# A planner's durations of a norm, and a new table for its ties, in a fused Mamba and MLP kernel

## The chip, the cores and the metric

The kernel runs on one core of a Trainium2 chip. The metric is the time of one execution on the device, in microseconds. A time given as a result is the median of several executions. A profile is one further execution, recorded by the hardware profiler: its span runs from the first to the last instruction.

TensorE (PE in the views) does the matmuls, and PEld is its loading of weights. VectorE is DVE, ScalarE is ACT, GpSimd is POOL, and SyncE is SP, which here only issues DMA transfers. Each engine has a queue of its own and takes its instructions in the order of the program. Engines wait for each other by semaphores.

## The reference

The input is 8 images of 384 channels and 32 by 32 points, so 1024 tokens each. A first branch is a state-space layer with an MLP, a second is an MLP with binarised weights whose outputs are quantised. Cut to what matters (the names are shortened):

```python
# 1: state space and MLP, all 8 images
t = layernorm(ln_c(x)) * ln_w + ln_b               # over 384 channels
xm, z = split(t @ in_proj_w.T)                     # 768 each
xc = silu(causal_conv(xm, 3 taps) + conv_b)
dt, Bm, Cm = split(xc @ x_proj_w.T)                # 24, 16, 16
dt = softplus(dt @ dt_proj_w.T + dt_proj_b)
h[l] = exp(dt[l] * A) * h[l-1] + dt[l] * xc[l] * Bm[l]   # 768 x 16 states, 1024 steps
y = (sum_n h * Cm + xc * D) * silu(z)
t = y @ out_proj_w.T
x = x + gelu(t @ mlp_w1.T + mlp_b1) @ mlp_w2.T + mlp_b2
# 2: per image, for the first 5 images (the other 3 pass through)
h = quantise(ln_t(x) @ sign(W1 - group mean).T + b1)     # 1536; absmax over the image
x = x + quantise(gelu(h) @ sign(W2 - group mean).T + b2)
```

## The kernel before

Everything is float32. An image is worked in two halves of 512 tokens (`T`), with the channels on the 128 partitions. Per image b there are a front part `s1` (norm, input projection, convolution, `dt`), the scan `s2`, an output part `s3` (output projection and MLP), and for b < 5 a second MLP `ffn`. What passes between the parts goes through DRAM.

The scan runs as exponentials on ScalarE (`da`), products on GpSimd (`u`, L992), prefix scans on VectorE (L1017) and sums over the 16 states on TensorE (`py`, L956). It takes most of the time of those three engines. The projections (`p_in`, `p_z`, `p_out`, `p_h`, `p_o`, `p_y`: L568) take most of TensorE's.

**Who orders the work.** The parts are not run as they are written. Each operation is recorded by `Plan.add` with an engine, a planned cost in microseconds, and what it reads and writes. When all are recorded, `Plan.run` plays them through once, on the host, when the program is built. It keeps a clock of its own for each engine, takes at each step the engine that can start earliest, lets `choose` pick one of the operations that are ready there, and emits it. So the planned costs decide nothing but the order of each engine's queue, and the host for those operations that may run on two engines (the `others` of `add`). The chip then follows that order with its true durations.

Where several operations are ready, `rank` sorts them: by a class for the part of the kernel, by the image, and then by the order of recording. The last is disturbed on purpose, by the table `TURNS` (L93), which has one number for each 100 us (`STRETCH`) of the planner's clock and 0 past its end:

```python
at = int(now / STRETCH)
turn = TURNS[at] if at < len(TURNS) else 0
...
by = turn & 0xFFFF
return (*first, op.prio[2] + (turned(op.prio[2], by) if by else 0))
```

`turned` makes a shift between -16 and +16 out of the operation's number and `by`, as a hash does. The bits above 65535 are flags for the stretch. `LATE_FRONTS` ranks the front parts behind the output parts. `DVE_SCANS` and `POOL_SCANS` let VectorE or GpSimd take the operations of the scan first; without them they come behind other work that is ready. `ACT_STAGES` holds ScalarE to operations outside of the scan that need no change of its function table.

If the planner's TensorE would be idle for more than 0.7 us (`IDLE`), it puts in filler matmuls of 256 columns, `spare` (L478), whose results nobody reads.

**The norm** (`norm`, 26 groups of it: 16 in the front parts, 10 in `ffn`) is a round trip over all engines, and TensorE has four steps of it. `total` adds three blocks of channels, on GpSimd in two additions (L655, L656) or on VectorE in one reduction (L659). `p_mean` (L667) is a matmul with ones, which sums over the partitions and spreads the sum. VectorE subtracts the mean (L670), ScalarE squares, and `p_var` (L626, helper `columns`) sums the squares in 12 small matmuls on a quarter of the array each. An eviction brings `var` to SBUF and `p_turned` (L681) transposes it. VectorE adds the epsilon (L685), GpSimd takes the power -0.5 (L687), `p_r` (L644, helper `spread`) spreads it in 4 matmuls, and VectorE multiplies (L691). The 4 matmuls `p_r` can't start before the power is there, and whatever stands behind them in TensorE's queue waits as well.

PSUM has three buffers (`mm`) for the matmuls' results; a matmul can't start until one of them has been emptied by ScalarE or VectorE (`affine`: L597, L599, L604, L606).

Of the kernel before, what the change touches and what calls it, by code (L numbers as in the profile page):

```python
# [35 lines left out]
KC = C // P  # L36
# [8 lines left out]
T = 512  # L45
# [26 lines left out]
MM = 0.859  # L72
# [18 lines left out]
STRETCH, REACH = 100, 16  # L91
LATE_FRONTS, DVE_SCANS, POOL_SCANS, ACT_STAGES = 1 << 16, 1 << 17, 1 << 18, 1 << 19
TURNS = (  # L93
    59965, 29935, 54697, 25830, 41556, 52704, 5806, 54013, 24204, 552223,
    25982, 47623, 34875, 16007, 24111, 42172, 43083, 15421, 638691, 11540,
    33479, 220645, 233617, 13861, 59336, 49176, 14182, 227647, 59245, 317456,
)


# [9 lines left out]
def c_act(n):  # L109
    return 0.2 + n * 0.00084  # L110


def c_dve(n):
    return 0.17 + n * 0.00102
# [90 lines left out]
class Plan:  # L205
# [12 lines left out]
    def add(self, engine, cost, emit, r=(), w=(), claim=(), table=None, size=0, others=None,  # L218
            land=1.6, rate=350e3, lag=None, tiled=False):
        op = Op()  # L220
        op.engine, op.cost, op.emit, op.table = engine, cost, emit, table
        op.others, op.settle = others or {}, None
        op.size, op.land, op.prio = 0.03 + size / rate, land - 0.1, (*self.prio, len(self.ops))
        op.next, op.ready, op.tiles, op.tiled = [], 0.0, [], tiled
        op.lag = LAG.get(engine, 0.0) if lag is None else lag
        op.slack = SLACK if self.prio[0] < 0 else 0.0
        deps = set()

        def parts_of(t):
            t, part = t if isinstance(t, tuple) else (t, None)  # L230
            if t not in op.tiles:
                op.tiles.append(t)
                if t.ring is not None:
                    t.left += 1
            if part is None:
                if None not in t.parts:
                    t.parts[None] = [None, []]
                return list(t.parts.values())
            if part not in t.parts:
                whole = t.parts.get(None)  # L240
                t.parts[part] = [whole[0], list(whole[1])] if whole else [None, []]
            return [t.parts[part]]

        for t in claim:
            t.left += 1
            op.tiles.append(t)
        for t in r:
            for p in parts_of(t):
                if p[0] is not None:
                    deps.add(p[0])  # L250
                p[1].append(op)
        for t in w:
            for p in parts_of(t):
                if p[0] is not None:
                    deps.add(p[0])
                deps.update(p[1])
                p[0], p[1] = op, []
        deps.discard(op)
        op.wants = len(deps)
        for d in deps:  # L260
            d.next.append(op)
        self.ops.append(op)
        return op
# [154 lines left out]
class Layer:  # L418
# [198 lines left out]
    def norm(self, t, eps, scale):  # L617

        nc, add = self.nc, self.plan.add
        def columns(src, name):  # L620
            p = self.piece("mm", [P, TG], name)

            def emit():
                for k in range(KC):
                    for g in range(G):
                        nc.tensor.matmul(  # L626
                            p.real[g * DQ : (g + 1) * DQ, :], self.ones[:, :DQ],
                            src.real[:, k, g * TG : (g + 1) * TG],
                            start=(k == 0), stop=(k == KC - 1),
                        )  # L630

            add("PE", 0.79, emit, r=[src], w=[p], tiled=True)
            return p

        def spread(src, name, turned=False):
            p = self.piece("mm", [P, T], name)

            def emit():
                for g in range(G):
                    if turned:  # L640
                        by, of = src.real[:, g : g + 1], self.ident
                    else:
                        by, of = self.ident[:, g * DQ : g * DQ + 1], src.real
                    nc.tensor.matmul(  # L644
                        p.real[:, g * TG : (g + 1) * TG], by.to_broadcast([P, P]), of,
                        start=True, stop=True,
                    )

            add("PE", 0.89, emit, r=[src], w=[p])
            return p  # L650

        total = self.piece("sq", [P, T], "total")

        def in_two():
            nc.gpsimd.tensor_add(total.real, t.real[:, 0, :], t.real[:, 1, :])  # L655
            nc.gpsimd.tensor_add(total.real, total.real, t.real[:, 2, :])  # L656

        def at_once():
            nc.vector.tensor_reduce(  # L659
                total.real, t.real.rearrange("p k l -> p l k"), AX.X, ALU.add  # L660
            )

        add("POOL", 2.5, in_two, r=[t], w=[total], others={
            "DVE": (c_dve(KC * T) + 0.02, at_once)
        })
        p_mean = self.piece("mm", [P, T], "p_mean")
        add("PE", MM, lambda: nc.tensor.matmul(  # L667
            p_mean.real, self.ones, total.real, start=True, stop=True
        ), r=[total], w=[p_mean])
        add("DVE", c_dve(KC * T) + 0.05, lambda: nc.vector.scalar_tensor_tensor(  # L670
            t.real, p_mean.real.unsqueeze(1).to_broadcast([P, KC, T]), -1.0 / C, t.real,
            ALU.mult, ALU.add,
        ), r=[p_mean], w=[t])

        sq = self.piece("sq", [P, KC, T], "sq")
        self.act(lambda: sq.real, lambda: t.real, AF.Square, c_act(KC * T), r=[t], w=[sq])
        p_var = columns(sq, "p_var")
        var = self.piece("rstd", [P, TG], "var")
        self.affine(lambda: var.real, lambda: p_var.real, [p_var], [var], scale=scale, n=TG)
        p_turned = self.piece("mm", [P, G], "p_turned")  # L680
        add("PE", 0.14, lambda: nc.tensor.matmul(  # L681
            p_turned.real, var.real, self.ident[:, ::DQ], start=True, stop=True
        ), r=[var], w=[p_turned])
        rstd = self.piece("root", [P, G], "rstd")
        add("DVE", 0.15, lambda: nc.vector.tensor_scalar_add(rstd.real, p_turned.real, eps),  # L685
            r=[p_turned], w=[rstd])
        add("POOL", 1.0, lambda: nc.gpsimd.tensor_tensor(  # L687
            rstd.real, rstd.real, self.power.to_broadcast([P, G]), ALU.pow
        ), w=[rstd])
        p_r = spread(rstd, "p_r", True)  # L690
        add("DVE", c_dve(KC * T), lambda: nc.vector.tensor_mul(  # L691
            t.real, t.real, p_r.real.unsqueeze(1).to_broadcast([P, KC, T])
        ), r=[p_r], w=[t])
# [738 lines left out]
```

## Time and profile before

| what | time |
|---|---|
| median of 3 runs | 3130.09 us (3128.02 to 3130.24) |
| the profiled execution | 3132.08 us |
| its span | 3130.3 us |
| granted TensorE clock, mean | 0.993 |
| fillers `spare` (L478), 119 matmuls | 58.6 us busy on TensorE |
| `p_var`, 26 groups of 12 matmuls | 22.0 us busy |
| `p_r`, 26 groups of 4 matmuls | 31.2 us busy |
| `p_mean`, 26 matmuls | 29.4 us busy |
| `total` on GpSimd, first and second addition | 1.28 and 1.27 us each |
| `total` on VectorE | 1.91 us each |

A matmul in float32 leaves two records in the trace, as it passes the array twice. Busy time of a group is the time in which at least one of its instructions ran. The span is less than the time of the execution by what lies around the first and the last instruction, 1.8 us here.

### The profile page before, as it was taken

The page shows a single profiled execution, that of the slowest core. Times are in us where ns is not written, and L with a number is a line of the kernel's source. Part 1 is how long each engine was busy: PE and PEld are TensorE (multiplying, and loading weights), DVE is VectorE, ACT ScalarE, POOL GpSimd, SP SyncE. Part 2 cuts the span into 40 slices and gives each one's busy share as a digit, 9 for nine tenths or more (in the row PEclk, how much of TensorE's full clock was granted, in tenths as well). Part 3 has the DMA queues.
Part 4 walks back from the last instruction along what each step waited for, and adds up shares of the span by engine and source line. Part 5 has one row for each costly group of instructions (what it writes and reads, how often), then busy time and mean ns, then how long its engine had stood idle before and what let it go on. Part 6 is the DMA issues. An engine that isn't in the chain of part 4 may idle for free.

```text
span 3130.3 us, 32297 instructions
## 1 busy us (share of the span) xinstructions
PE 3049.4 (97%) x10202; PEld 1243.8 (40%) x10202; DVE 2599.5 (83%) x2053; ACT 2019.1 (65%) x2406; POOL 2802.1 (90%) x1095
## 2 busy tenths in 40 slices
PE   9899999999999999999999999999999999999999
PEld 4334333333333444434343334343334444333334
DVE  4787888999987889878799888898788988798880
ACT  4887787776576566667666665666745556666562
POOL 2889888999999998999989998999999999999880
PEclk9999999999999999999999999999999999999999
DMA  7999778777787667777679675886877756756442
GB/s 231 305 312 314 241 255 282 272 251 254 256 318 241 207 202 259 280 263 259 202 256 319 206 231 194 298 276 211 269 250 229 238 187 220 243 187 211 155 152 73
DMA packets 348969, 751.76 MB, mean 240 GB/s; under 512 B 36480, under 2 KB 113792, under 8 KB 339584
## 3 DMA queue, kind: packets, MB, share of 16 engines
q1 hardware_dynamic: 348368, 749.61, 71.9%
q8 instruction: 82, 1.34, 0.2%
q14 instruction: 87, 0.71, 0.1%
q10 hardware_dynamic: 432, 0.09, 0.0%
HBM read 569.21 MB, written 180.36 MB: 239 GB/s over the span
## 4 chain that ended last, share of the span: by engine, by line
PE 53%; DVE 6%; DMA 5%; ACT 5%; POOL 4%; issue 2%; SPq 0%; DVEq 0%; POOLq 0%; ACTq 0%
PE p_y L568 16%; PE p_o L568 11%; PE p_h L568 9%; PE py L956 7%; PE p_out L568 5%; POOL u L992 3%; DVE u L1017 2%; PE p_in L568 2%; DVE da L1017 2%; PE p_z L568 2%; ACT da L584 1%; ACT L584 1%; DMA w_b<-in_mlp_w 1%; DMA w<-in_mlp_w 1%; DMA w_n<-bin_w 1%
## 5 line engine op out<-in xcount | busy, mean ns | idle before, releaser
L584 ACT ACTIVATE da<-dt_r,a_neg 128x1024 f32<-128x1024 f32 (+1 forms) x960 | 898.2, 944 | 559.4 <-DVE u L1017 292.1
L992 POOL TENSOR_TENSOR u<-dtx_r,bc 128x2048 f32<-128x2048 f32 (+1 forms) x360 | 1186.4, 3311 | 75.7 <-PE py L956 38.8
L1017 DVE TENSOR_TENSOR_SCAN u<-da,u 128x1024 f32<-128x1024 f32 (+1 forms) x436 | 871.2, 2009 | 165.7 <-POOL u L992 77.7
L992 POOL TENSOR_TENSOR u<-u,bc 128x2048 f32<-128x2048 f32 (+1 forms) x274 | 900.0, 3290 | 74.4 <-DVE u L1017 68.0
L568 PE MATMUL p_h<-t,w_b 128*128 128x512 f32 x1152 | 513.1, 597 | 10.7 <-DMA w_b<-in_mlp_w 5.0
L568 PE MATMUL p_o<-g,w 128*128 128x512 f32 x1152 | 512.3, 597 | 7.5 <-DMA w<-in_mlp_w 5.7
L1017 DVE TENSOR_TENSOR_SCAN da<-da,dtx_r 128x1024 f32<-128x1024 f32 (+1 forms) x192 | 380.4, 2014 | 51.1 <-POOL dtx_r L992 31.4
L992 POOL TENSOR_TENSOR dtx_r<-dtx_r,bc 128x2048 f32<-128x2048 f32 (+1 forms) x120 | 397.0, 3312 | 1.8
L568 PEld LDWEIGHTS p_o<-g,w 128*128 128x128 f32 x1152 | 214.6, 190 | 299.7 <-issue 271.1
L568 PE MATMUL p_y<-gf,w_n 128*128 128x512 f32 x720 | 323.5, 601 | 9.3 <-DMA w_n<-bin_w 6.0
L568 PEld LDWEIGHTS p_h<-t,w_b 128*128 128x128 f32 x1152 | 213.9, 190 | 298.1 <-issue 259.8
L568 PE MATMUL p_y<-tn,w_b 128*128 128x512 f32 x720 | 318.9, 597 | 3.2 <-DVE rstd L685 2.5
L956 PE MATMUL py<-u,fold 128*32 128x512 f32 x2304 | 303.2, 625 | 0.0
L1017 DVE TENSOR_TENSOR_SCAN da<-da,u 128x1024 f32<-128x1024 f32 (+1 forms) x140 | 280.8, 2037 | 11.7 <-ACT da L584 10.8
L584 ACT ACT_TABLE_LOAD x213 | 273.3, 1283 | 5.5 <-DMA dt_r<-dt_d 1.8
L568 PE MATMUL p_out<-yg,w 128*128 128x512 f32 x552 | 245.5, 596 | 2.1 <-DMA w<-in_out_proj_w 1.3
L568 PE MATMUL p_in<-t,w_f 128*128 128x512 f32 x504 | 230.6, 606 | 12.6 <-issue 5.2
L568 PE MATMUL p_z<-t,w_f 128*128 128x512 f32 x504 | 227.1, 599 | 2.0 <-issue 1.0
L568 PEld LDWEIGHTS p_y<-gf,w_n 128*128 128x128 f32 x720 | 134.1, 191 | 196.0 <-issue 173.4
L568 PEld LDWEIGHTS p_y<-tn,w_b 128*128 128x128 f32 x720 | 134.4, 190 | 184.5 <-issue 167.0
L1037 DVE TENSOR_TENSOR dtx_r<-da,bc 128x1024 f32<-128x1024 f32 x144 | 170.8, 1214 | 0.1
L599 ACT ACTIVATE g<-p_h,v_vecs 128x512 f32<-128x512 f32 x159 | 107.5, 678 | 89.9 <-PE p_h L568 89.4
(131 smaller groups left out, 3152.4 us busy)
## 6 DMA issues: line engine op xcount, KB each, us to landing
dtx_r<-dtx_d SPq DMA_DIRECT2D x72, 1024.0 KB, 5.9
dt_r<-dt_d SPq DMA_DIRECT2D x144, 512.0 KB, 5.1
w_b<-in_mlp_w SPq DMA_DIRECT2D x192, 192.0 KB, 3.5
w<-in_mlp_w SPq DMA_DIRECT2D x96, 384.0 KB, 3.4
w_f<-in_in_proj_w SPq DMA_DIRECT2D x168, 192.0 KB, 4.4
y_d<-y SPq DMA_DIRECT2D x120, 256.0 KB, 4.9
gf<-y_d SPq DMA_DIRECT2D x60, 512.0 KB, 6.3
xc_d<-xc SPq DMA_DIRECT2D x48, 512.0 KB, 6.1
```

The lines of the kernel that those rows point to most:

```text
L568: self.nc.tensor.matmul(p.real, w.real[:, w0 + k, :], t.at(k0 + k), start=start and k == 0, stop=stop and k == n - 1,)
L584: lambda: self.nc.scalar.activation(out(), in_(), func, **{k: v() if callable(v) else v for k, v in kw.items()}),
L599: nc.scalar.activation(out(), in_(), AF.Identity, bias=bias, scale=scale)
L956: nc.tensor.matmul(py.real[g * DQ : (g + 1) * DQ, :], self.fold, hc, start=False, stop=(q == NQUAD - 1), skip_group_check=True,)
L992: nc.gpsimd.tensor_mul(u.real[:, x], t.real[:, x], row.real.unsqueeze(2).to_broadcast([P, n, 2]))
L1017: da=da, in_u=in_u: nc.vector.tensor_tensor_scan(to(i), da.real[:, i, :], in_u(i), state.real[:, col : col + 1] if half else 0.0, ALU.mult ...
L1037: nc.vector.tensor_mul(u.real[:, 0, :, t], da.real[:, 0, :], cq.real)
```

## The change

Four planned costs of the norm are changed, and with them the cost of `total` on VectorE, and the table of ties is replaced by one with 29 numbers in place of 30. No operation is added, removed or altered in shape; what the planner makes of them may differ.

```diff
 TURNS = (
-    59965, 29935, 54697, 25830, 41556, 52704, 5806, 54013, 24204, 552223,
-    25982, 47623, 34875, 16007, 24111, 42172, 43083, 15421, 638691, 11540,
-    33479, 220645, 233617, 13861, 59336, 49176, 14182, 227647, 59245, 317456,
+    1467, 19521, 11834, 15884, 418848, 355954, 44882, 19020, 0, 58934,
+    440381, 41878, 59848, 768481, 6782, 6493, 42608, 22157, 465781, 3132,
+    641679, 27278, 604202, 3404, 13756, 5072, 104706, 15493, 80705,
 )
...
-            add("PE", 0.79, emit, r=[src], w=[p], tiled=True)
+            add("PE", 0.68, emit, r=[src], w=[p], tiled=True)
...
-            add("PE", 0.89, emit, r=[src], w=[p])
+            add("PE", 0.98, emit, r=[src], w=[p])
...
-        add("POOL", 2.5, in_two, r=[t], w=[total], others={
-            "DVE": (c_dve(KC * T) + 0.02, at_once)
+        add("POOL", 2.64, in_two, r=[t], w=[total], others={
+            "DVE": (1.91, at_once)
         })
...
-        add("PE", MM, lambda: nc.tensor.matmul(
+        add("PE", MM + 0.08, lambda: nc.tensor.matmul(
             p_mean.real, self.ones, total.real, start=True, stop=True
         ), r=[total], w=[p_mean])
```

`MM` is 0.859 us, and `c_dve(KC * T) + 0.02` comes to 1.76 us. Flags stand in the table of before for the stretches from 900 us (`ACT_STAGES`), 1800 (`LATE_FRONTS`, `ACT_STAGES`), 2100, 2200 and 2700 (`LATE_FRONTS`, `DVE_SCANS`) and 2900 (`POOL_SCANS`). In the new one they stand for those from 400 and 1000 (`DVE_SCANS`, `POOL_SCANS`), 500 (`LATE_FRONTS`, `POOL_SCANS`), 1300 (`LATE_FRONTS`, `DVE_SCANS`, `ACT_STAGES`), 1800 (`LATE_FRONTS`, `DVE_SCANS`, `POOL_SCANS`), 2000 and 2200 (`LATE_FRONTS`, `ACT_STAGES`) and 2600 and 2800 (`LATE_FRONTS`).

## The prediction

> **What bounds the kernel now.** I read the page's busy times first, then the busy times in stretches of 100 us, then the planner's filler matmuls in the same stretches, the TensorE timeline around the stalls, and the waits.
>
> ```profile
> PE 3049.4 (97%) x10202; PEld 1243.8 (40%) x10202; DVE 2599.5 (83%) x2053; ACT 2019.1 (65%) x2406; POOL 2802.1 (90%) x1095
> PE 53%; DVE 6%; DMA 5%; ACT 5%; POOL 4%; issue 2%; SPq 0%; DVEq 0%; POOLq 0%; ACTq 0%
> L584 ACT ACT_TABLE_LOAD x213 | 273.3, 1283 | 5.5 <-DMA dt_r<-dt_d 1.8
> ```
>
> TensorE is busy for 3049.4 of 3130.3 us, so all idle time there is 80.9 us. The chain of waits (second line; it reaches back to 787 us only) is mostly TensorE too. The order of TensorE's queue is the planner's, and nothing overtakes in it. An edit that changes no shape can therefore gain only out of three stores: the 80.9 us of idle, the filler matmuls (L478), and the matmuls that ran at half clock. The next view has, for each stretch, its length, the busy time and instruction count of PE, PEld, DVE, ACT and POOL, the granted clock, the DMA share and GB/s.
>
> ```profile
> 0.00:100.00 100.00, 88.47 (x353) 44.15 (x354) 45.99 (x71) 52.03 (x70) 36.86 (x35) 0.97 0.75 251
> 100.00:200.00 100.00, 94.15 (x328) 36.82 (x327) 81.33 (x84) 83.06 (x118) 92.92 (x66) 0.97 0.93 308
> 200.00:300.00 100.00, 93.62 (x360) 44.02 (x359) 79.95 (x85) 85.94 (x135) 86.57 (x61) 0.98 0.93 313
> 300.00:400.00 100.00, 94.41 (x340) 36.36 (x338) 85.22 (x79) 77.74 (x111) 88.91 (x49) 0.91 0.76 244
> ...
> 700.00:800.00 100.00, 91.98 (x388) 37.53 (x387) 95.16 (x68) 67.80 (x79) 99.32 (x32) 0.98 0.74 251
> ...
> 1000.00:1100.00 100.00, 100.00 (x308) 40.01 (x310) 80.20 (x49) 58.22 (x63) 97.29 (x33) 1.00 0.68 224
> ...
> 2500.00:2600.00 100.00, 98.28 (x337) 43.89 (x340) 88.70 (x61) 63.95 (x65) 98.08 (x29) 1.00 0.57 188
> ```
>
> Idle time is early (11.5, 5.9, 6.4 and 5.6 us in the first four) and at 700 to 800 (8.0 us); later stretches have 0 to 4. GpSimd is over 90% busy from 600 us nearly to the end, so it follows close behind. The fillers, in the same stretches (PE busy, PEld busy):
>
> ```profile
> 0.00:100.00 100.00, 11.22 (x46) 9.27 (x46) 0.97 0.75 251
> 100.00:200.00 100.00, 3.74 (x14) 2.49 (x14) 0.97 0.93 308
> 200.00:300.00 100.00, 18.71 (x78) 14.31 (x78) 0.98 0.93 313
> ...
> 2500.00:2600.00 100.00, 13.32 (x58) 10.78 (x58) 1.00 0.57 188
> ...
> sum 3131.00, PE 58.57 PEld 44.68; mean PE 1.83 PEld 1.40
> ```
>
> Each filler leaves two records, so 119 of them took 58.57 us: 0.49 us each, time in which the planner expected no work. Two stalls of the norm's round trip, in the TensorE timeline (start, length, instruction, idle before it):
>
> ```profile
> 87.85 0.28 PE L681 MATMUL p_turned<-ident,var 128*128 128x4 f32 x2
> ...
> 92.17 1.53 PE L644 MATMUL p_r<-ident,rstd 128*128 128x128 f32 x8 [3.78 <-POOL rstd L687]
> ```
> ```profile
> 754.09 1.28 PE L644 MATMUL p_r<-ident,rstd 128*128 128x128 f32 x8 [2.26 <-POOL rstd L687]
> 755.16 1.92 PE L667 MATMUL p_mean<-total,small 128*128 128x512 f32 x2
> 756.87 1.06 PE L478 MATMUL spare<-small 128*128 128x256 f32 x2
> 759.61 2.84 PE L568 MATMUL p_in<-t,w_f 128*128 128x512 f32 x6 [1.68 <-ACT t L599]
> ```
>
> The spread (L644) waits for a power on GpSimd (L687) that needs the transposed sums (L681). Where the queue has only 0.4 us of other work between the two, TensorE waits for the rest.
>
> **What the skill says of this.** "TensorE: Matmul & The Clock Gate", Part 1, What's actually happening: the clock is gated by recent activity in free windows of about 3.4 us, half speed after an idle one, full after a busy one. The trace agrees: from 310 to 320 us the granted clock was 0.60, from 330 to 340, after a gap of 4.56 us, 0.74. Over the span it is 0.993, so 0.7% of 3130, some 22 us of full-speed time, were withheld. A stall thus costs more than itself: that of 4.56 us was followed by about 5 us of half-speed matmuls (each at 0.85 us instead of 0.43), 2 to 3 us more. "ScalarE: Activation LUTs", What ACT_TABLE_LOAD costs, states 1283 ns for a load and about 1380 ns of drain beside it. The trace has the same 1283 ns and no such drain: idle ahead of all 213 loads is 5.5 us, and the activation after the one at 86.33 us starts 0.02 us after its end. I go by the trace, 1.283 us.
>
> **The five durations (L632, L649, L663 to L664, L667).** They only feed the planner's clock. The chip's instructions stay as they are: 26 groups each of sums, spread and mean. Removed and added work: 0. By the trace the reduction on VectorE takes 1.907 us (planned 1.76, now 1.91) and two additions on GpSimd 1.28 + 1.27 plus a short gap (2.5, now 2.64), so the plan comes nearer there. A shift of 0.1 us per norm moves every later tie and every host chosen.
>
> **The new table (L93 to L97).** It reorders all five queues from about 40 us on; counts come from the two built programs, durations from the trace.
> - Fillers: 119 to 102, by 17. By place in the queue, 69 to 39 in the first 300 us of work, 3 to 8 from there to 1000, 2 to 3 up to 2300, 43 to 49 from 2300 to 2700, 2 to 3 behind it. 17 x 0.49 = 8.4 us less on TensorE. A filler hides nothing but idle time; its going is a gain only if the work behind it is ready, else it returns as a wait.
> - Round trips. For each point where TensorE needs a tile made from its own earlier result, I summed the matmul work queued between, and set it against the trip's own need (about 1.0 us for an eviction, 2.3 for sums to spread: 0.15 + 1.02 and hand-overs; 3.0 for spread, multiply and affine). Before, 17 points fall short, by 14.2 us in all; after, 13 by 8.3. The pairs at 82 and 729 us of queue (the stalls shown) are gone; new are a spread at 261 with 0.5 us of cover and one at 271 with 2.1. So 5.9 us less. The three worst spreads of before were short by 6 us and stalled for 1.51 + 3.78 + 2.26 = 7.6, so the model is not too large; but fillers and shortages partly count the same idleness, so I take half: 3 us.
> - Half clock: the two stalls removed each sat in a half-speed window, 1.7 us each; the new ones may bring as much. From -3.4 to +3.4; I take 0.
> - ScalarE: 213 to 184 table loads, 29 x 1.283 = 37 us less. ScalarE is 65% busy and only 5% of the chain, so at most a tenth or so, 4 us, could show; evictions come earlier by it. I take 0, as it is already in the two lines above. Ten evictions (6 of z, 4 of g) go from ScalarE to VectorE, 3 of xc come back, and two more totals go to VectorE: 6 x 0.69 + 4 x 0.75 - 3 x 0.81 + 1.9 = 7 us on VectorE (83% busy), hidden by its idle 17%; if that cover is gone the scans start later by as much.
> - GpSimd: one pair of additions less, 2.6 us, and nothing else; SyncE: the same 2255 issues in a new order. Every load is as large as before; how often one comes late is redrawn (stalls on weight loads total about 20 us before). I bound it by -8 and +12, and take 0.
> - The scans' place: the twelfth group of y sums stood behind 474 us of work and 69 fillers (508 us), now 470 and 40 (490); the 48th 1585 plus 36 (1621), now 1585 plus 23 (1608); the last 3005 plus 58, now 3005 plus 50. So scans are not pushed back, and the tail behind the last one is the same 75 us of matmuls.
>
> Sum: -8.4 - 3 = -11.4 on the profiled execution's 3132.1 (span 3130.3 and 1.8 outside), 3120.7. The median of the runs is 2 us lower, 3130.1: that gives 3118.7. I say 3120.
>
> **Rivals.** A measurement of this kernel tells a change from none at about 0.2%, 6.3 us: 3123.8 to 3136.4 is "the same".
> - The stalls are conserved (chance 0.25): the trace has some 50 us in gaps over 0.8 us that no filler foresaw, waits for weights, gelu and evictions. A new order has its own, and fillers that go become waits. For: the gap of 4.56 us at 330 us and the 3.30 us for w_n at 978 us lie where no round trip is short. Against: round trips are better covered. The net is about -4 on 3132: 3128.
> - Slower (0.28): scans ahead of evictions. The new table sets its scan-first flags in five stretches (400, 500, 1000, 1300, 1800 us), before in four (2100, 2200, 2700, 2900). There VectorE and GpSimd take scans of 2 to 4 us ahead of the gate and convolution work that empties TensorE's three PSUM buffers; the flagged stretches of before, later and poorer in such work, idled for 0 to 3 us. At 400 to 600 us it meets the front work of the next batches. Price by the stall at 330 us: 4.6 plus 2.5 of half clock, 7 us; four such of the five make 28, so 3120 + 28 = 3148. It decides from three on (+21, net +10).
> - A larger gain (part of the first 0.47): the full 5.9 x 1.2 = 7 us of round trips, 3.4 of clock and 4 of ScalarE on top of 8.4: 23 us, 3107.
> - That the order on the chip is not as planned can't be: it is fixed when the program is built.
>
> **How the numbers follow.** Fewer fillers as a gain 0.47, all of it faster or nearly; conserved 0.25; slower 0.28. Of the likeliest a little, 0.03, ends within 0.2%, and of the conserved 0.02 ends beyond it, to either side: faster 0.45, same 0.26, slower 0.29. The range of the likeliest alone is 3107 to 3126; to leave out 2 in 10, with a tenth on each side, it becomes 3106 to 3147.
>
> **What would show it.** Right: fillers near 50 us in all, some 20 in the first 300; TensorE idle at 75 to 82 us in all; idle at 700 to 800 us below 4; clock 0.993 or more. Table loads 184 at 1283 ns. Wrong: idle of 100 us or more on TensorE with granted clock at 0.990 or less, with waits for VectorE or ScalarE evictions at 400 to 600, 1000 or 1300 us; or fillers gone but as much new idle in the first 300 us.

## The result, and the profile after

The changed kernel took 3137.86 us, the median of 5 runs, against 3129.82 for the kernel before in the same rounds. The ratio is 1.0035, with a 95% interval from 1.0021 to 1.0050: slower by 8 us, where about 10 were to be gained. A second set of 5 runs (the first experiment below) gave 1.0037 [1.0023, 1.0050].

The page of its profile (span 3142.7 us; busy time and share of the five engines, the chain of waits by engine, the table loads):

```profile
PE 3049.4 (97%) x10168; PEld 1239.1 (39%) x10168; DVE 2617.2 (83%) x2062; ACT 1979.9 (63%) x2370; POOL 2800.1 (89%) x1092
PE 59%; DVE 13%; DMA 8%; ACT 8%; POOL 7%; issue 5%; SPq 1%; DVEq 0%; POOLq 0%; ACTq 0%
...
L584 ACT ACT_TABLE_LOAD x184 | 236.1, 1283 | 6.2 <-DMA dt_r<-dt_d 3.0
```

TensorE is busy exactly as long as before, 3049.4 us, although 17 fillers are gone: they took 6.4 us less, and the other matmuls, at a mean clock of 0.990 in place of 0.993, as much longer. Its idle time rose from 80.9 to 93.3. The busy times in stretches of 100 us say where (columns as before):

```profile
0.00:100.00 100.00, 89.42 (x358) 42.65 (x358) 43.97 (x72) 51.80 (x69) 36.23 (x35) 0.97 0.78 257
100.00:200.00 100.00, 91.58 (x324) 35.69 (x323) 88.81 (x91) 85.42 (x121) 94.89 (x67) 1.00 0.89 295
200.00:300.00 100.00, 82.25 (x289) 32.18 (x287) 80.45 (x77) 71.54 (x111) 72.74 (x50) 0.90 0.81 276
300.00:400.00 100.00, 92.42 (x324) 37.38 (x323) 79.90 (x75) 75.06 (x113) 86.00 (x52) 0.90 0.82 272
...
700.00:800.00 100.00, 95.90 (x390) 40.56 (x389) 92.48 (x70) 75.47 (x86) 90.83 (x34) 0.98 0.79 268
```

From 200 to 300 us TensorE now idles for 17.7 us in place of 6.4, ScalarE and GpSimd lose some 14 us of work each, and the granted clock is 0.90. At 700 to 800 us the forecast came true: 4.1 us idle in place of 8.0. The fillers (PE busy, PEld busy) of the same profile:

```profile
0.00:100.00 100.00, 11.79 (x48) 9.50 (x48) 0.97 0.78 257
100.00:200.00 100.00, 0.00 (x0) 0.00 (x0) 1.00 0.89 295
200.00:300.00 100.00, 5.19 (x14) 2.83 (x14) 0.90 0.81 276
...
sum 3143.00, PE 52.18 PEld 38.61; mean PE 1.63 PEld 1.21
```

They fell from 33.7 to 17.0 us in the first 300, as counted. What came in their place stands in the timeline around the longest stall (start, length, engine, instruction, count, idle before it):

```profile
271.98 4.24 POOL L992 TENSOR_TENSOR u<-u,bc 128x1024 f32<-128x1024 f32 x2
...
273.62 0.16 DVE L1196 TENSOR_REDUCE mean<-p_means 128x5 f32<-128x10 f32 x1
...
273.81 10.77 DVE L1197 TENSOR_SCALAR mean<-mean 128x5 f32<-128x5 f32 x1
...
276.16 8.40 POOL L992 TENSOR_TENSOR u<-dtx_r,bc 128x1024 f32<-128x1024 f32 x4
...
284.49 2.33 DVE L1017 TENSOR_TENSOR_SCAN da<-da,dtx_r 128x512 f32<-128x512 f32 x2
...
286.74 1.20 DVE L1039 TENSOR_TENSOR dtx_r<-da,bc 128x1024 f32<-128x1024 f32 x1
...
287.98 0.16 ACT L1031 COPY state<-da 128x2 f32<-128x2 f32 x1 [9.62 <-DVE dtx_r L1039]
288.12 1.48 ACT L584 ACTIVATE sq<-t 128x1536 f32<-128x1536 f32 x1
...
289.65 1.51 PE L626 MATMUL p_var<-sq,small 128*32 128x128 f32 x24 [9.49 <-ACT sq L584]
```

An operation on 5 numbers per partition, L1197, took 10.77 us. It scales the group means of the binarised weights; the change doesn't touch it, and in the profile of before its two instances took 0.19 and 0.25 us. It ends 0.03 us after GpSimd's last product in that row (276.16 + 8.40 = 284.56, and 273.81 + 10.77 = 284.58). The scans and a product behind it on VectorE wait for it, ScalarE waits 9.62 us for that product (L1039) and has the square of a norm next, and TensorE waits 9.49 us for that square.

### The profile page after: what moved, and what is told of

It reads as the page before. It is cut to its first block, busy times and chain, and to the rows that moved or that the text cites. A ratio compares the mean times of both kernels' runs of the same rounds, so it can differ in the third digit from the quotient of the medians.

```text
span 3142.7 us, 32220 instructions
## 1 busy us (share of the span) xinstructions
PE 3049.4 (97%) x10168; PEld 1239.1 (39%) x10168; DVE 2617.2 (83%) x2062; ACT 1979.9 (63%) x2370; POOL 2800.1 (89%) x1092
## 4 chain that ended last, share of the span: by engine, by line
PE 59%; DVE 13%; DMA 8%; ACT 8%; POOL 7%; issue 5%; SPq 1%; DVEq 0%; POOLq 0%; ACTq 0%
PE p_y L568 13%; PE p_h L568 12%; PE p_o L568 11%; PE py L956 7%; POOL u L992 6%; DVE u L1017 5%; PE p_in L568 5%; PE p_out L568 4%; DVE da L1017 3%; PE p_z L568 3%; ACT da L584 3%; DMA w_b<-in_mlp_w 2%; ACT L584 2%; DMA dt_r<-dt_d 1%; PE p_dt L828 1%
## 5 line engine op out<-in xcount | busy, mean ns | idle before, releaser
L568 PE MATMUL p_h<-t,w_b 128*128 128x512 f32 x1152 | 512.7, 597 | 14.4 <-DMA w_b<-in_mlp_w 10.9
L568 PE MATMUL p_in<-t,w_f 128*128 128x512 f32 x504 | 233.1, 610 | 16.7 <-DVE xc L763 4.9
L584 ACT ACT_TABLE_LOAD x184 | 236.1, 1283 | 6.2 <-DMA dt_r<-dt_d 3.0
L599 ACT ACTIVATE y<-p_y,v_vecs 128x512 f32<-128x512 f32 x137 | 93.3, 682 | 120.8 <-PE p_y L568 91.5
```

The costliest lines, as they stand in the source:

```text
L568: self.nc.tensor.matmul(p.real, w.real[:, w0 + k, :], t.at(k0 + k), start=start and k == 0, stop=stop and k == n - 1,)
L584: lambda: self.nc.scalar.activation(out(), in_(), func, **{k: v() if callable(v) else v for k, v in kw.items()}),
L599: nc.scalar.activation(out(), in_(), AF.Identity, bias=bias, scale=scale)
```

## The experiments

**The changed kernel again (e1), and with the means scaled out of PSUM (e2).** The edit of e2 swaps the two operations on the means, so that the scaling reads PSUM and the reduction is the one from SBUF to SBUF. All queues keep their order, but for the two instructions themselves.

```diff
-            nc.vector.tensor_reduce(mean.real, p_mean.real, AX.X, ALU.add)
-            nc.vector.tensor_scalar_mul(mean.real, mean.real, -1.0 / (gs * kt * P * DQ))
+            nc.vector.tensor_scalar_mul(sums.real, p_mean.real, -1.0 / (gs * kt * P * DQ))
+            nc.vector.tensor_reduce(mean.real, sums.real, AX.X, ALU.add)
 
-        add("DVE", 0.4, means, r=[p_mean], w=[mean])
+        add("DVE", 0.4, means, r=[p_mean], w=[mean, sums])
```

> The changed kernel once more, for a second profile. Theory P (port): the 10.8 us that the tiny scaling of the means (L1197, VectorE, SBUF to SBUF) took at 274 us in its first profile is a block by GpSimd's products that run back to back beside it; it depends on a hair of timing, so the executions fall into two groups, near 3137 with a short L1197 (below 3 us) and near 3144 with one of 8 to 11 us. Theory O (order): L1197 stretched only because the profile drew it so; its length has no part in the time, and the five timings lie within 3 us of each other whatever it is.

> The means are scaled as they are read from PSUM and reduced afterwards, so no VectorE operation there has all its operands in SBUF with a scalar; the order of all queues stays. Theory P: neither of the two operations takes over 0.5 us in any profile, no 9 us gap of TensorE near 290 us, no execution above 3139; median 3130 to 3137, so 1 to 7 us below the changed kernel in the same rounds. Theory O: the reduction now takes as long as the scaling did, and the median is within 2 us of the changed kernel's. If all is well with L1197 and the median still stands at 3136 to 3138, the excess over before is in the waits of the first 600 us.

**The same edit in the kernel before (e3).**

> The same edit in the kernel before, whose two L1197 took 0.19 and 0.25 us. Theory P: within 1.5 us of the kernel before (3128.5 to 3131.5). Theory O: the same. A move of over 3 us either way would say that the edit itself (a buffer of sums held longer, two small operations in the other order) costs or gains, and then e2 can't be read as it stands.

Measured, against the kernel before in the same rounds: e1 1.0037 [1.0023, 1.0050]; e2 1.0006 [0.9997, 1.0014], median 3131.5 of 13 runs; e3 0.9995 [0.9987, 1.0003]. In e1's profile L1197 took 10.76 us once more. Its five times, 3138.8 to 3146.6, don't fall into two groups, so that part of theory P, a hair of timing, has nothing for it: the block came in both profiles of this order. Nor do they lie within 3 us, as theory O had it. In e2 neither operation takes over 0.17 us, as P said, and the median is within its bounds; but one run was at 3140.7, above the 3139 that it gave, and the median is 10.9 us below that of e1, more than its 1 to 7. The edit alone does nothing that can be told to the kernel before (e3). The timeline of e2 in the same stretch:

```profile
273.42 0.15 DVE L1196 TENSOR_SCALAR sums<-p_means 128x10 f32<-128x10 f32 x1
...
273.60 0.17 DVE L1197 TENSOR_REDUCE mean<-sums 128x5 f32<-128x10 f32 x1
273.68 2.34 DVE L1017 TENSOR_TENSOR_SCAN da<-da,dtx_r 128x512 f32<-128x512 f32 x2
...
275.97 8.45 POOL L992 TENSOR_TENSOR u<-dtx_r,bc 128x1024 f32<-128x1024 f32 x4
...
278.09 1.48 ACT L584 ACTIVATE sq<-t 128x1536 f32<-128x1536 f32 x1
...
280.25 0.86 PE L626 MATMUL p_var<-sq,small 128*32 128x128 f32 x24
```

GpSimd runs the same row of products, VectorE passes in 0.17 us, the square stands 10 us earlier, and the stall is gone. So the one operation carries the whole excess: from 1.0037 to 1.0006, some 10 us. And without it the change is worth nothing that can be told, where about 10 us had been forecast. Both need an explanation.

Where the forecast gain went can be read from the profiles of before and of e2. Below stand the busy times of e2's engines; then, for the first 600 us, all busy times and those of the fillers (columns as in the tables of stretches), first of before, then of e2; then TensorE's waits for the norm's power (us in all, times, longest), of before and of e2:

```profile
PE 3041.7 (97%) x10168; PEld 1238.0 (40%) x10168; DVE 2606.7 (83%) x2062; ACT 1980.2 (63%) x2370; POOL 2800.3 (90%) x1092
...
0.00:600.00 600.00, 564.12 (x2021) 238.32 (x2022) 464.11 (x472) 447.97 (x624) 483.04 (x292) 0.97 0.83 277
0.00:600.00 600.00, 33.68 (x138) 26.07 (x138) 0.97 0.83 277
...
0.00:600.00 600.00, 554.75 (x1966) 227.23 (x1967) 466.58 (x467) 434.75 (x606) 479.40 (x284) 0.97 0.83 277
0.00:600.00 600.00, 21.76 (x80) 15.54 (x80) 0.97 0.83 277
...
PE p_r L644 <- POOL rstd L687: 7.5, 3, 3.8
PE p_r L644 <- POOL rstd L687: 2.8, 3, 1.5
```

In the first 600 us e2 has 11.9 us of fillers less (33.68 to 21.76) and 9.4 us of idle time more (35.9 to 45.3). The norm's round trips did become shorter: over the span, TensorE's waits for GpSimd fell from 11.2 to 4.2 us. But its waits for VectorE and ScalarE rose from 36.6 to 47.3, of which the first 600 us alone have 19.2 and 33.0.

**What GpSimd blocks (e4, e5).** In the kernel before, a tiny operation follows each of the 84 gate products on VectorE. In e4 the three kinds alternate; e5 has the first kind at all 84 places. The planned costs, and so the order, stay.

```diff
+                kind, self.probes = self.probes % 3, self.probes + 1
+                if kind == 0:
+                    nc.vector.tensor_scalar_mul(x[:, 0], x[:, 0], 1.0)
+                elif kind == 1:
+                    nc.vector.tensor_scalar_mul(x[:, 1], py.real[:, :5], 1.0)
+                else:
+                    nc.vector.tensor_mul(x[:, 2], x[:, 2], x[:, 3])
```

> The kernel before with one tiny VectorE operation of 128x5 put in behind each of 84 gate products (L973), in turn of three kinds: a scaling from SBUF to SBUF, the same from PSUM, and a product of two SBUF tiles; no other order changes. Theory P (port): the scaling from SBUF stands still while GpSimd runs products back to back: its 28 times spread from 0.2 to over 5 us, several of them end within 0.05 us of the end of a GpSimd product, and their mean is over 1 us; those from PSUM stay at 0.15 to 0.25. Of the two-tile product P says nothing sure: a full block would hold it at most to the end of the product running, 2 to 4 us. Theory G (general): any tiny VectorE operation can be held up by GpSimd, so all three kinds show it alike. Theory N: none of the three exceeds 0.5 us, and L1197 is a case of its own.

> The same with all 84 operations of the SBUF to SBUF kind. Theory P: VectorE is 83% busy and GpSimd 90%, so most of what an operation waits for delays the scans: at a mean of 2 us for each, 84 x 2 = 168 us on VectorE, and some 60 to 170 us more time (3190 to 3300). If the mean wait is below 0.5 us: less than 20 us more. Theory N: 84 x 0.2 = 17 us on VectorE, hidden, within 6 us of before.

The view of e4's tile (line, engine, operation, count: least, median and greatest time in ns, first and last start):

```profile
L981 DVE TENSOR_SCALAR probe<-probe x28: 161/1550/3601, 135.3 to 2696.8; 128x5 f32<-128x5 f32 x28
L983 DVE TENSOR_SCALAR probe<-py x28: 150/153/158, 171.0 to 2736.1; 128x5 f32<-128x5 f32 x28
L985 DVE TENSOR_TENSOR probe<-probe x28: 278/2255/8267, 208.4 to 2756.6; 128x5 f32<-128x5 f32 x28
```

and of e5's:

```profile
L979 DVE TENSOR_SCALAR probe<-probe x84: 155/1884/16243, 133.2 to 2825.7; 128x5 f32<-128x5 f32 x84
```

GpSimd was running an operation at the start of each of the 84 in e4, so the kinds met the same neighbour. The same scaling takes 0.15 us whenever it reads PSUM, and 1.76 us on average (49.3 us for 28) when it reads SBUF. Of those 28, 27 end 26 to 49 ns after the end of a GpSimd instruction; only the shortest doesn't. The product of two SBUF tiles is held up as well: 28 of 28 end 17 to 26 ns after one, up to 8.3 us. So theory G falls (PSUM is exempt), N falls, and P stands; its reserve about the two-tile product was not needed. e4 took 2.32% [1.43, 3.22] longer than before, from two runs that lie 23 us apart. In e5, the 202 us that the 84 operations took cost 4.33% [3.89, 4.76], some 134 us: about two thirds came out at the end. Most of the 84 get through when the product that is running ends (the longer ones take 4.1 us), but 5 wait for over 5 us and one for 16.2, through several products that follow each other. L1197 of the changed kernel is one of these few.

Being held up is not new with the change, though. The profile of before has one case, three sums of two SBUF tiles at the very start, of which one took 1.195 us where the median is 0.178; it ends 0.04 us after the end of a GpSimd addition:

```profile
L508 DVE TENSOR_TENSOR join<-ident x3: 169/178/1195, 7.1 to 8.3; 128x24 f32<-128x24 f32 x2, 128x32 f32<-128x32 f32 x1
```

**Each half of the change alone (e6: durations, e7: table).** The edits are the hunks of the diff above.

> The five durations of the change with the old table. By the planner's own clock this plan ends at 3210 us, that of before at 3072 and the changed one at 3066. Theory T (a table belongs to its durations): the chip follows the plan in the large, 3130 + 100 to 140, so 3230 to 3270; the time is lost as idle TensorE and fillers. Theory R (the chip doesn't follow the plan at all; ties are worth some 10 us): within 20 us of before, 3110 to 3150.

> The new table with the durations of before. Planned end 3174. Theory T: 3130 + 80 to 110, so 3210 to 3240. Theory R: 3110 to 3150. Together with e6 this says whether either half of the change could have been tried alone.

The planned end is where the planner's clock for TensorE stands when the kernel has been built. The median of the kernel before differs between the rounds, from 3129.8 to 3135.0, so each kernel stands beside before in its own rounds:

| kernel | planned end, us | measured median, us | difference | difference for before, same rounds |
|---|---|---|---|---|
| before | 3072.3 | 3131.7 and 3135.0 | | 59.3 and 62.6 |
| changed, means from PSUM (e2) | 3065.9 | 3131.5 | 65.6 | 59.3 |
| old durations, new table (e7) | 3174.4 | 3241.7 | 67.3 | 62.6 |
| new durations, old table (e6) | 3210.3 | 3279.6 | 69.3 | 62.6 |

Theory R falls and theory T holds, though both medians lie above its ranges, by 10 and 2 us: e6 is 4.65% [4.34, 4.95] slower than before, e7 3.44% [3.14, 3.74]. So the old table with five durations moved by 0.08 to 0.15 us makes a much slower kernel. The time goes where T said: in e6's profile fillers (280 of them, 139.3 us) and idle time (126.9) take 266.2 us together, in place of 139.5. L1197 has no part in it: it takes 1.49 us at most in these two. The planner's clock orders plans that differ by 100 us rightly. But its distance from the chip is 5 to 7 us greater for each of these three than for before, and the change's planned gain was 6.5.

**No fillers (e8: before, e9: changed with the means from PSUM).**

```diff
-                    self.fill()
```

> The kernel before, its order kept to the letter, without its 119 filler matmuls (58.6 us busy on TensorE). Theory S (my step: each filler is 0.49 us of TensorE time that work behind it could use): up to 58 us less, at least 20: 3072 to 3110. Theory I (fillers lie in time that would be idle anyway, the work behind them isn't ready): no gain, within 6 us of before (3124 to 3136), with idle time of TensorE up by 45 to 60 us; or slower by up to 15, where the clock falls to half in the gaps (granted clock below 0.990).

> The changed kernel with the means scaled from PSUM, without its 102 fillers. Theory S: 20 to 50 us less than 3131.5. Theory I: 3126 to 3146, and no further from e8 than e2 was from before (3 us): the number of fillers says nothing of the time.

e8: 1.0043 [1.0028, 1.0058], median 3144.0. e9: 1.0030 [1.0020, 1.0040], median 3139.4, which is 4.6 us below e8, a little more than the 3 us allowed. Theory I in its second form: without fillers the kernel is slower by 14 us. The busy times of e8's profile, and its stretches, with nothing else changed:

```profile
PE 3017.4 (96%) x9964; PEld 1205.7 (38%) x9964; DVE 2602.5 (83%) x2053; ACT 2019.3 (64%) x2406; POOL 2802.2 (89%) x1095
...
0.00:100.00 100.00, 78.50 (x298) 36.52 (x299) 44.77 (x70) 49.59 (x66) 34.24 (x34) 0.95 0.75 248
100.00:200.00 100.00, 92.90 (x310) 34.62 (x309) 77.53 (x81) 80.10 (x113) 89.56 (x63) 0.93 0.90 295
200.00:300.00 100.00, 82.56 (x285) 31.29 (x284) 82.73 (x87) 84.51 (x134) 86.48 (x63) 0.93 0.92 308
...
2500.00:2600.00 100.00, 87.30 (x283) 33.16 (x282) 87.68 (x62) 57.88 (x61) 96.00 (x29) 0.93 0.57 186
```

In the first and third stretch the fillers had taken 11.2 and 18.7 us. Without them TensorE is busy for 10.0 and 11.1 us less (from 88.5 to 78.5 and from 93.6 to 82.6): hardly any work moves up into the first gap, and in the third stretch, too, most of the time stays empty, while the clock falls from 0.97 and 0.98 to 0.95 and 0.93. Over the span idle time is 124.8 us, less than the 139.5 that fillers and idle time took before. But the other matmuls take 3017.4 us in place of 2990.8 (3049.4 - 58.6), as the clock is 0.985 in place of 0.993: by an estimate from these two means, 0.8% of the span, some 25 us more of full-speed time were withheld. That costs more than the 14.7 us gained.

## Why the prediction was wrong

- **Range and direction.** 3120 was forecast and faster held likelier; it is 3137.9, inside the range, in the part that belonged to the rival on the slower side, with another cause than that rival's. That the range holds it is luck.
- **The step that failed: "17 x 0.49 = 8.4 us less on TensorE".** It took filler time for time that work behind it could use, with the proviso that else it returns as a wait. Most of it returned. What counts, as long as the clock stays the same, is fillers and idle time together: 139.5 us before (58.6 + 80.9), 137.1 in e2's profile (51.9 + 85.2), and 145.5 after. The other matmuls take the same in before and e2, 2990.8 and 2989.8 us. The 2.4 us that are left are no gain: e2's profile is of the fastest of its 13 executions, and that of before 2 us above its median. What came in place of the fillers are waits for VectorE and ScalarE, 10.7 us more. e8 asks another question, as there no order changes: it shows that fillers where they stand gain more by the clock than they cost.
- **The price of a queue that wasn't read.** VectorE's work was costed by kind and count, "hidden by its idle 17%". That a 0.2 us operation can take 10.8 by its place beside GpSimd was nowhere in the sum; the profile of before had one small hint of it (L508), and neither of its two L1197. e1 to e3 show its price here, about 10 us, and e4 which kinds are held. Without it the sum would still have been wrong, by the step above.
- **Round trips: -3, right in kind.** The two stalls shown are gone, and 700 to 800 us idles for 4.1 us. In e2 TensorE waits 7.0 us less for GpSimd, even more than the 5.9 of which half was taken. But new waits came at other points, so the first rival, that stalls are conserved, describes e2 best: its 3128 stands against 3131.5.
- **Half clock: 0, right without L1197.** The mean clock of e2's profile is that of before, 0.993.
- **The slower rival: seen at one place of five.** In all three profiles of the new order TensorE waits 4.76 us for the convolution (L763) at 500 to 513 us, where VectorE runs four scans and two products ahead of it; half-clock windows follow. The four such stalls of its price did not come. Its time was near the measured one, its reason was not. In the changed kernel's profile:

```profile
505.26 4.81 DVE L1017 TENSOR_TENSOR_SCAN da<-da,state,dtx_r 128x512 f32<-128x512 f32 x4
...
513.02 2.93 PE L568 MATMUL p_in<-t,w_f 128*128 128x512 f32 x3 [4.76 <-DVE xc L763]
```

- **Table loads and host changes at 0: nothing contradicts it.** 184 loads at 1283 ns, 37 us less of ScalarE, and e2 gains nothing that can be told.
- **The signs.** Of those of "right", the fillers came as said (52.2 us, 17.0 in the first 300) and the idle time did not (93.3). Of "wrong", the second form came in the changed kernel, nearly: in the first 300 us fillers lost 16.7 us and idle time grew by 13.0, most of it L1197's stall. In e2 it grew by 5.3 there, and the rest came between 300 and 600 us. Of the first form only the clock of 0.990 came.
- **Open.** Why the kernel before lies 5 to 7 us nearer to its plan than the three others isn't settled; that it had been the luckiest of many is an argument and not shown. Why VectorE and ScalarE deliver later than the plan of e2 has it, at so many points of the first 600 us, was not taken apart either.

## What to carry to other kernels

Idle time that is stuffed with fillers is still idle time: compare plans by fillers and idle time together, with the granted clock beside them, and don't take fillers out before a run without them is faster. When a scheduler's plan is judged by its own clock, find first by how much that clock misses the chip from plan to plan, in the same rounds, and don't expect a smaller planned gain to arrive. In the trace, look for tiny VectorE operations with a long greatest time: where GpSimd is busy, let such an operation read PSUM, or reduce where it would scale, instead of working from SBUF to SBUF.

## What the runs showed of the hardware

Beside a busy GpSimd, a VectorE scaling of 128x5 from SBUF to SBUF took 1.8 to 2.4 us on average and up to 16.2, a product of two SBUF tiles of that size 2.4 us and up to 8.3; reading PSUM the scaling took 0.15 us, 0.158 at most. The Trainium skill, "SBUF — State Buffer", Who interferes with whom, has the rule: VectorE and GpSimd share a pair of ports under an exclusive lock, which a one-source operation in a two-port mode takes, and one with two SBUF inputs against a GpSimd operation that reads SBUF. The trace agrees for the three kinds of e4; which mode an operation ran in is not in it.

The page has the loser wait for the other's whole instruction; here L1197 waited past the ends of five products in a row, 10.77 us. Each time GpSimd's next product had started 0.06 to 0.07 us before the last one ended. That is not enough to explain it: in e4 and e5, GpSimd's next instruction overlapped the end of the last one at 17 ends at which the held operation stayed held, and at 107 at which it got through. Where GpSimd's next instruction started only after the end, it always got through (32 cases). What decides the rest is open.

Two cases were not held up at all, and why isn't shown. The ten sets of operations of 128x1 in the second MLP (L1241 to L1245), also SBUF to SBUF, took 0.14 to 0.16 us in both profiles, nearly all beside a running GpSimd operation. And the first L1197 of the kernel before and of the changed one started 0.03 us after GpSimd's power had (L687), and took 0.19 us.
